# Two transformer blocks on one core: row tests moved to where rows are made, a second query buffer, weight casts on GpSimd, and other places and steps for the Strassen stage's sums, loads and offsets

## The chip, the cores and the metric

The kernel runs on one NeuronCore of a Trainium2 chip. The metric is the device time of one execution in microseconds. Before the change three runs gave a median of 2838.97 us (2838.28 to 2842.82).

## The reference

The input x is 16 sequences of 256 rows with 512 channels, with a context of the same shape. Two blocks follow each other. All arithmetic is in float32.

```python
def block0(x, context, xa_mask):                     # 16 heads of 32
    q = layer_norm(x, qn_w, qn_b) @ q_w
    k, v = split(layer_norm(context, cn_w, cn_b) @ kv_w)
    attn = where(xa_mask, -max, q @ k.T * scale);  attn = softmax(attn)
    x = x + (attn @ v) @ proj_w + proj_b
    h = layer_norm(x, n2_w, n2_b)
    return x + gelu(h @ fc1_w + fc1_b) @ fc2_w + fc2_b    # 512 -> 2048 -> 512

def block1(x, context):
    mask0 = 1.0 - all(x == 0, axis=2)                # per row
    x1 = layernorm(x + mha(x, x, mask0, causal=True))
    mask1 = 1.0 - all(x1 == 0, axis=2)               # per row
    x2 = layernorm(x1 + mha(x1, context, mask1, causal=False))
    z = relu(x2 @ fc1_w.T + fc1_b) * mask0
    return layernorm(x2 + (z @ fc2_w.T + fc2_b) * mask0)
```

In `mha` the mask multiplies Q, K, V and the result, and a number of valid columns is counted from the first row's energies that differ from zero.

## The kernel before

The 16 sequences are worked on as 8 groups (NG) of two sequences, so a group has N = 512 rows, in G = 4 row tiles of 128. A float32 product is made of three matmuls in the format fp32r: every operand is held as a high part (its leading bits, `h`) and a low part (`l` = value - high part), and `mm3` issues high x high, high x low and low x high. The helpers `split`, `split_sb` and `split_lazy` (L119 to L142) make the two parts. In most places ScalarE casts the high part (`nc.scalar.copy`) and VectorE subtracts.

The stages follow each other. Times are of the profiled execution.

- **Phase 1** (to about 711 us): attention of block 0. `Attention.stream` yields, head by head, scores (L409), exponentials (L434, ScalarE, with minima that VectorE made), transposes of the exponentials (L450), their copy to `pt` (L453, ScalarE), and per unit of 4 heads the mixing with V (L466). `weave` interleaves it on PE with a `fill` of projections (`feed`), in proportion to costs that both yield. The last group is woven with `last()`, which also opens the feed forward part: `Mlp0.begin` loads the rows of group 0, normalizes them, makes the first weights and the first operands.
- **Up stage** (about 711 to 1061 us): h @ fc1_w with a seven-product Strassen-Winograd scheme over 2x2 blocks. One step n takes 7 products of 12 matmuls; a group has NS = 4 steps. `sums` makes the four block sums of the operand, `write` puts each of the seven operands as high and low part into one of eight slots as soon as the product that read the slot has been issued. Results go through GELU into `ho` and are stored to DRAM as `hid`.
- **Down stage** (about 1054 to 1458 us): hidden @ fc2_w the same way, 32 steps of 84 matmuls (L1005). In step n, `sums_down(n+1)` makes the sums of the next hidden tile (GpSimd L786 and L788, VectorE L787 and L789) into tile `x2`, which has one buffer; seven `write`s follow between the products; `hidden(n+2)` loads the hidden tile after that (L978), alternately into the tiles `raw` and `x0`. At the first step of a group `residual(g)` loads the group's rows into tile `x1` (L1017) and GpSimd adds the offset `b_fc2` to them (L1018). At the last step `end` adds the seven products into these rows (L1033 to L1050) and stores them (L1052). In the last step of all, `after_up` is called after products 1, 6, 7 and 4; each call loads one row tile of block 1's first group (L1306) and transposes it.
- **Weights of the down stage**: `weigh(2, m)` makes four block differences on GpSimd (L835 to L838, tile `diff`) and splits them, m = 0 to 7. Even m use the `diff` of one pool, odd m that of another. The last two are called just before the down stage.
- **Block 1** (from about 1458 us): self attention of the 8 groups, then cross attention of the 8 groups, then the feed forward part. `front(n, t)` loads a row tile of the job after next (L1306), transposes it, and calls `nonzero` (L1181 to L1186), the row test: VectorE compares 128x512 elements with zero and accumulates a maximum per row, which is the mask. For job 0 `feed(0)` makes these tests. `halves(pool, 0)` gives the buffer `qk0` for one chunk of queries: `split` fills it, `att.keep` stores it to DRAM (L379) so that `build` can load it in the layout of the scores. Chunks of keys have two buffers, those of queries one. `Weight.load` (L174 to L192) loads a chunk of weights, ScalarE casts its high part (L185) and GpSimd subtracts (L186).

Only PE's order is written out by hand (`tc.manual_schedule(engines={PE})`). The other engines' queues and SP's, which issues the DMAs, are put in order when the program is built: the planner follows a model of time, takes an instruction when it becomes ready there, and prefers the one that the program emitted first where several are ready. [...] The pools' tiles wait for the last use of the tile that had the buffer before.

## Time and profile before

The profiled execution took 2842.86 us, of which the span from its first to its last instruction is 2841.0 us.

| | us |
|---|---|
| median of three runs | 2838.97 |
| profiled execution | 2842.86 |
| its span | 2841.0 |
| PE idle in the span | 153.4 |
| row tests L1184: 64, each | 0.68 |
| copies pt L453 of 512 columns: 512, each | 0.595 |
| high parts of weights in block 1 on ScalarE L185, each | 0.62 |

In lines of the profile that list groups or timelines, `out<-in` are the program's names of tiles without buffer numbers, then come the shapes, and in brackets the idle time of the engine just before the instruction and what ended it. A line of waits gives who waited (engine, tile, line), for what, the total time, how often, and the longest. In the lines of stretches each engine has its busy time and its number of instructions; the last three numbers are TensorE's granted clock as a share of full speed, the busy share of the DMA engines, and GB/s.

### The profile page before, as it was taken

What the parts mean: (1) busy time and instruction counts of PE and PEld (TensorE: products, weight loads), DVE (VectorE), ACT (ScalarE), POOL (GpSimd) and SP (SyncE); (2) the same over time, 40 slices, a digit from 0 to 9 for tenths busy, and PEclk for the clock granted to TensorE, in tenths of its full rate; (3) what the DMA queues carried; (4) which work ended last, traced back from release to release, by engine and by line L of the source; (5) the groups of instructions that cost most, each with busy time, mean ns of one, the idle gap of its engine ahead of it and who ended that gap; (6) DMA issues with size and microseconds to landing.
All of it is one profiled execution on the core that took longest, in us unless ns stands there. A gap on an engine that the chain in (4) does not pass through costs nothing.

```text
span 2841.0 us, 56513 instructions
## 1 busy us (share of the span) xinstructions
PE 2687.6 (95%) x18970; PEld 2263.3 (80%) x18970; DVE 2013.1 (71%) x5722; ACT 1840.9 (65%) x5320; POOL 932.9 (33%) x943
## 2 busy tenths in 40 slices
PE   7999999998999989899979999998999999999998
PEld 5777777776899988898977777777777777777787
DVE  7666666757665567787876777776777776776887
ACT  4877777778655553333337777777777777778632
POOL 6122221206311044545441222234333323234533
PEclk9999999999999999999989999999999999999999
DMA  6566565655333343433465556667666665555321
GB/s 228 172 189 186 173 180 170 186 164 151 137 121 133 127 164 132 136 131 138 137 205 176 180 184 186 180 191 216 200 193 186 179 181 177 175 172 169 96 94 60
DMA packets 287664, 465.40 MB, mean 164 GB/s; under 512 B 36240, under 2 KB 188304, under 8 KB 279184
## 3 DMA queue, kind: packets, MB, share of 16 engines
q1 hardware_dynamic: 287376, 461.78, 51.7%
q8 instruction: 153, 2.51, 0.4%
q14 instruction: 135, 1.11, 0.1%
HBM read 284.97 MB, written 176.69 MB: 162 GB/s over the span
## 4 chain that ended last, share of the span: by engine, by line
PE 65%; DMA 11%; DVE 11%; ACT 5%; issue 4%; POOL 2%; SPq 1%; POOLq 0%; ACTq 0%; DVEq 0%
PE ps_v L259 15%; PE ps_p L259 14%; PE ps_pt L450 8%; PE down L1005 6%; PE ps_z L466 5%; PE ps_s L409 4%; PE up_sc L899 4%; DMA x<-xd 3%; PE up_pt L899 3%; ACT e L434 3%; PE up_mm L899 2%; DMA d<-qk 2%; DMA xd<-x 2%; PE ps_t L278 2%; DVE c_t L142 1%
## 5 line engine op out<-in xcount | busy, mean ns | idle before, releaser
L434 ACT ACTIVATE e<-e,mn 128x256 f32<-128x256 f32 (+1 forms) x1024 | 488.2, 481 | 85.1 <-DVE mn L424 83.9
L453 ACT COPY pt<-ps_pt 128x512 f32<-128x512 f32 (+1 forms) x768 | 422.1, 555 | 130.9 <-PE ps_pt L450 124.2
L450 PE MATMUL ps_pt<-ident,e 128*128 128x128 f32 x2816 | 437.0, 273 | 10.4 <-ACT pt L453 9.7
L450 PEld LDWEIGHTS ps_pt<-ident,e 128*128 128x128 f32 x2816 | 336.1, 141 | 52.3 <-ACT pt L453 15.7
L409 PE MATMUL ps_s<-stack 97*128 97x256 f32 (+1 forms) x1536 | 332.8, 298 | 34.2 <-ACT e L434 26.5
L409 PEld LDWEIGHTS ps_s<-stack 97*128 97x128 f32 (+1 forms) x1536 | 267.9, 190 | 98.4 <-ACT e L434 42.7
L1283 POOL TENSOR_TENSOR x<-x,zz 128x256 f32<-128x256 f32 x128 | 95.4, 746 | 593.6 <-DVE zz L1276 565.5
L1005 PE MATMUL down<-w_h,c_t 128*128 128x256 f32 x900 | 265.2, 295 | 24.3 <-DVE c_t L142 24.1
L434 ACT ACTIVATE e<-ps_s,mn 128x256 f32<-128x256 f32 x512 | 244.9, 498 | 65.2 <-DVE mn L420 59.2
L238 POOL TENSOR_TENSOR rstd<-rstd,nhalf 128x1 f32<-128x1 f32 x192 | 127.0, 668 | 472.4 <-DVE rstd L237 425.0
L1005 PE MATMUL down<-w_h,x_t 128*128 128x256 f32 x868 | 254.9, 294 | 18.8 <-ACT x_t L141 18.8
L1005 PE MATMUL down<-w_l,x_t 128*128 128x256 f32 x868 | 253.6, 292 | 0.0
L424 DVE CUSTOM_DVE_ANT_0 e<-mb,ps_s 128x256 f32<-128x256 bf16 x512 | 192.5, 415 | 76.3 <-PE ps_s L409 73.4
L259 PE MATMUL ps_p<-x_t,q_h 128*128 128x512 f32 x640 | 213.9, 415 | 3.2 <-DVE qk L128 3.2
L420 DVE TENSOR_REDUCE mn<-ps_s 128x2 f32<-128x512 f32 x256 | 174.3, 682 | 57.8 <-PE ps_s L409 56.0
L141 ACT CAST x_t<-sums 128x512 fp32r<-128x512 f32 x156 | 93.5, 620 | 178.0 <-DVE sums L787 121.9
L466 PE MATMUL ps_z<-pt,v 128*32 128x256 f32 (+1 forms) x3072 | 201.5, 368 | 5.7 <-ACT pt L453 3.7
L1005 PEld LDWEIGHTS down<-w_h,c_t 128*128 128x128 f32 x900 | 181.9, 202 | 27.8 <-DVE c_t L142 27.8
L434 ACT ACTIVATION_READ_ACCUMULATOR e<-e,mn 128x1 f32 x1024 | 198.5, 194 | 0.0
L1005 PEld LDWEIGHTS down<-w_h,x_t 128*128 128x128 f32 x868 | 175.3, 202 | 20.6 <-ACT x_t L141 20.6
L424 DVE CUSTOM_DVE_ANT_0 e<-tri,ps_s 128x128 f32<-128x128 f32 (+1 forms) x512 | 157.8, 346 | 45.4 <-PE ps_s L409 41.9
L1005 PEld LDWEIGHTS down<-w_l,x_t 128*128 128x128 f32 x868 | 175.2, 202 | 0.0
(242 smaller groups left out, 7515.6 us busy)
## 6 DMA issues: line engine op xcount, KB each, us to landing
stack<-d SPq DMA_DIRECT2D x1152, 128.0 KB
d<-qk SPq DMA_DIRECT2D x192, 512.0 KB
hid<-ho SPq DMA_DIRECT2D x32, 1024.0 KB
raw<-hid SPq DMA_DIRECT2D x32, 1024.0 KB
x<-xd SPq DMA_DIRECT2D x128, 256.0 KB
xd<-x SPq DMA_DIRECT2D x96, 256.0 KB
xin<-in_x_dram SPq DMA_DIRECT2D x32, 256.0 KB
xin<-in_ctx_dram SPq DMA_DIRECT2D x32, 256.0 KB
```

What stands on the lines that cost most here:

```text
L238: nc.gpsimd.tensor_tensor(out=rstd[:, 1:2], in0=rstd[:, 0:1], in1=nhalf, op=ALU.pow)
L259: nc.tensor.matmul(ps, w[p], x[q], start=(k == 0 and i == 0), stop=(k == kc - 1 and i == 2))
L409: nc.tensor.matmul(ps[:, t, :], u.st[: self.rows, 0, j, ts(t, P)], u.st[: self.rows, 1, j, :], start=True, stop=True,)
L420: nc.vector.tensor_reduce(mn, ps, AX.X, ALU.min)
L424: nc.vector.tensor_tensor_reduce(out=e[:, at], in0=bias[t], in1=ps[:, t, : job.width[t]], scale=-SC, scalar=BIG, op0=ALU.add, op1=ALU.min, ...
L434: nc.scalar.activation(e[:, at], ps[:, t, :] if bias is None else e[:, at], AF.Exp, bias=mn[:, t : t + 1], scale=-1.0, accum_out=u.rs[:, t ...
L450: nc.tensor.transpose(pp[:, ts(x, P)], e[:, at : at + P], ident)
L453: nc.scalar.copy(pt[:, :n], pp[:, :n])
L466: nc.tensor.matmul(z[ts(j, D), w[0] * P :], job.v[u.i * NT + mc][:, u.c * P + j * D : u.c * P + (j + 1) * D], u.pt[j][:, x0 * P : (x0 + le ...
L899: nc.tensor.matmul(ps[:, mm, :], w[p][:, k, :], x[q][:, k, :], start=(first and mm == k == j == 0), stop=(k == 1 and j == 2), skip_group_c ...
L1005: nc.tensor.matmul(ps[:, t, :], x[p][:, mm, ts(t, P)], w[r][:, bo, :], start=(q == mm == t == j == 0), stop=(q == self.NS - 1 and mm == 1 ...
L1283: nc.gpsimd.tensor_tensor(out=xv, in0=xv, in1=zz, op=ALU.add)
```

## The change

It makes these edits:

- `Weight.load` can cast the high part on GpSimd (`pooled`); block 1 asks for it for all weights but those of job 0.
- The copy of `pt` goes to VectorE for the heads in `job.shared`: the last head of each unit, in the last group of phase 1 and in all cross jobs.
- `weigh(2, m)` uses the second `diff` only for m = 1. The last two calls move behind steps 0 and 1 of the down stage.
- `write` with an `own` engine (in `begin`) casts the high part on VectorE.
- `normal` is divided into `row` (load) and `normal`. In `begin` all rows are loaded first, with a yield of 12 passes, then normalized, with 3 passes each. In the up stage all four rows of a later group are loaded at step 0 into tile `raw`, and normalized in steps 1 and 2.
- `sums_down(0)` writes into two `xn` tiles and the second `diff` instead of `x2`.
- `residual` (loads) runs in the second step of a group (third for group 0), `offset` (GpSimd's additions) one step later.
- Row tests run in `end`, after the stores, and in `Mha.norm` of self attention, after the layer norm; those in `front` and `feed(0)` are gone.
- In the last down step all row tiles are loaded after product 1 and transposed after products 2, 5, 4 and 3.
- Chunks of queries get two buffers. The third row of the last norm table, fc2's offset, gets a tile of its own.

```diff
             for k in ks:
...
                 if self.gain is None:
-                    nc.scalar.copy(h, raw)
+                    if self.pooled:
+                        nc.gpsimd.tensor_copy(h, raw)
+                    else:
+                        nc.scalar.copy(h, raw)
                     nc.gpsimd.tensor_tensor(out=l, in0=raw, in1=h.bitcast(F32), op=ALU.subtract)
...
-            nc.scalar.copy(pt[:, :n], pp[:, :n])
+            if j in job.shared:
+                nc.vector.tensor_copy(pt[:, :n], pp[:, :n])
+            else:
+                nc.scalar.copy(pt[:, :n], pp[:, :n])
...
-            pool = self.pool if early or m % 2 == 0 else self.tmp
+            pool = self.tmp if not early and m % 2 and (way == 1 or m == 1) else self.pool
             diff = pool.tile([P, 4, 2 * P], F32, tag="diff", name="diff")
...
         def write(self, i, own=None):
-            split_lazy(
-                self.a[i],
-                *[x.rearrange("p (k n) -> p k n", n=self.W) for x in self.next[i]],
-                own or nc.vector,
-            )
+            h, l = [x.rearrange("p (k n) -> p k n", n=self.W) for x in self.next[i]]
+            if own is None:
+                split_lazy(self.a[i], h, l, nc.vector)
+            else:
+                nc.vector.tensor_copy(h, self.a[i])
+                own.tensor_tensor(out=l, in0=self.a[i], in1=h.bitcast(F32), op=ALU.subtract)
...
         def sums_down(self, n):
...
-            s = self.px.tile([P, 4, 2, self.W], F32, tag="x2", name="sums")
-            s = [s[:, i] for i in range(4)]
+            if n == 0:
+                s = [self.up_pool.tile([P, C], F32, tag="xn", name="sums") for _ in range(2)]
+                two = self.tmp.tile([P, 4, 2 * P], F32, tag="diff", name="sums")
+                two = two.rearrange("p (i m) n -> p i m n", m=2)
+                s = [x.rearrange("p (m n) -> p m n", m=2) for x in s] + [two[:, i] for i in range(2)]
+            else:
+                s = self.px.tile([P, 4, 2, self.W], F32, tag="x2", name="sums")
+                s = [s[:, i] for i in range(4)]
...
+            return x
+
+        def offset(self, x):
+            for t in range(G):
                 nc.gpsimd.tensor_tensor(
                     out=x[:, t, :], in0=x[:, t, :], in1=self.b_fc2, op=ALU.add
                 )
-            return x
...
                 for t in range(G):
                     nc.sync.dma_start(out=xd[1][g][ts(t, P), :], in_=x[:, t, :])
+                for t in range(G):
+                    junk = self.flat("junk").rearrange("p m n -> p (m n)")
+                    nonzero(junk, x[:, t, :], m0[:, g, t : t + 1])
...
             for t in range(G):
-                self.normal(0, t, xn[:, t, :])
-                yield 0.0
+                self.row(0, t, xn[:, t, :])
+            yield 12 * PASS
+            for t in range(G):
+                self.normal(xn[:, t, :])
+                yield 3 * PASS
...
-            self.weigh(2, self.NM - 2)
-            self.weigh(2, self.NM - 1)
...
-                if q == 0:
+                if q == (1 if g else 2):
                     xs[g] = self.residual(g)
+                elif q == (2 if g else 3):
+                    self.offset(xs[g])
                 if n + 1 <= last:
                     self.sums_down(n + 1)
...
-                    if n == last and i in (1, 6, 7, 4):
-                        after_up((1, 6, 7, 4).index(i))
+                    if n == last and i in (1, 2, 5, 4, 3):
+                        after_up((1, 2, 5, 4, 3).index(i))
                 self.at = self.next
+                if n < 2:
+                    self.weigh(2, self.NM - 2 + n)
...
                 layer_norm(pool, x, table[:, 0, :], table[:, 1, :], True)
+                if not self.cross:
+                    junk = pool.tile([P, C], F32, tag="t512", name="junk", bufs=3)
+                    nonzero(junk, x, m1[:, self.g, t : t + 1])
...
             x = job.x[:, t, :]
-            nc.sync.dma_start(out=x, in_=xd[2 if job.cross else 1][job.g][ts(t, P), :])
-            cost = transposed(job.x_t, x, t)
-            if n:
-                nonzero(pool, x, job.m[:, t : t + 1])
-            return cost
+            return transposed(job.x_t, x, t)
...
+        def after_up(step):
+            if step:
+                front(0, step - 1, False)
+            else:
+                for t in range(G):
+                    rows_of(0, t)
...
-            if n == 0:
-                for t in range(G):
-                    nonzero(pool, job.x[:, t, :], job.m[:, t : t + 1])
...
-                q, hl = halves(pool, 0)
+                q, hl = halves(pool, 0, 2)
```

`rows_of(n, t)` issues the load that `front` issued, and `front` calls it unless it is told that the rows are loaded already.

## The prediction

> **What bounds the kernel now.** I read the page's engine rows first, then the stretches of stages, the waits, and the timeline around the longest waits.
>
> ```profile
> span 2841.0 us, 56513 instructions
> PE 2687.6 (95%) x18970; PEld 2263.3 (80%) x18970; DVE 2013.1 (71%) x5722; ACT 1840.9 (65%) x5320; POOL 932.9 (33%) x943
> ```
>
> PE is the bound, so a gain can only come out of its gaps: 2841.0 - 2687.6 = 153 us[...]. Where they lie (us, PE, PEld, DVE, ACT, POOL, PEclk):
>
> ```profile
> 640.00:760.00 120.00, 103.93 (x789) 86.90 (x788) 89.99 (x247) 91.17 (x248) 67.30 (x74) 0.99 0.46 145
> 1040.00:1098.00 58.00, 42.71 (x310) 41.40 (x310) 44.45 (x52) 28.83 (x52) 31.66 (x26) 0.85 0.43 146
> 1098.00:1440.00 342.00, 313.17 (x2444) 308.80 (x2442) 274.76 (x308) 123.25 (x215) 175.26 (x118) 0.94 0.39 133
> 1440.00:1500.00 60.00, 48.70 (x254) 40.79 (x253) 39.44 (x102) 17.36 (x31) 18.70 (x21) 0.91 0.70 233
> 1920.00:2040.00 120.00, 105.22 (x759) 83.24 (x758) 85.06 (x367) 89.00 (x303) 54.81 (x51) 0.99 0.73 221
> 2040.00:2680.00 640.00, 611.86 (x4339) 481.27 (x4338) 453.88 (x1128) 488.77 (x1546) 211.74 (x207) 0.99 0.57 170
> ```
>
> Gaps are length less PE busy: 16.1 where phase 1 ends, 15.3 and 28.8 in the Strassen down stage, 11.3 where block 1 starts, 14.8 and 28.1 in cross attention. The last two stages together have 43 of the 153. The waits name the culprits:
>
> ```profile
> POOL x L1018 <- DMA x<-xd: 53.3, 7, 8.5
> DVE junk L1184 <- DMA x<-xd: 35.6, 30, 3.5
> PE ps_s L409 <- ACT e L434: 26.5, 22, 4.2
> ACT qk L127 <- DMA d<-qk: 24.4, 12, 4.0
> ```
>
> Three engines stand in order behind a transfer. GpSimd, in the down stage:
>
> ```profile
> 1124.15 1.29 POOL L786 TENSOR_TENSOR sums<-raw 128x512 f32<-128x512 f32 x1 [2.48 <-issue]
> 1125.40 1.74 POOL L788 TENSOR_TENSOR sums<-raw 128x512 f32<-128x512 f32 x1
> 1135.14 2.54 POOL L1018 TENSOR_TENSOR x<-x,b_fc 128x512 f32<-128x512 f32 x2 [8.00 <-DMA x<-xd]
> 1137.65 1.29 POOL L786 TENSOR_TENSOR sums<-raw 128x512 f32<-128x512 f32 x1
> ```
>
> The sums at 1137.65 wait behind an offset that waits for its load. The first offset of a group starts at 1135.14, 1182.79, 1231.04 and so on to 1372.02: 47.4 us a group. A group's 4 x 84 matmuls stand 0.12 us apart in PE's timeline, 40.3 us: 7 us are lost per group. And VectorE, in cross attention:
>
> ```profile
> 2088.24 0.69 DVE L1184 TENSOR_SCALAR_CACHE_REDUCE junk<-x 128x512 f32<-128x512 f32 x1 [3.46 <-DMA x<-xd]
> 2089.96 0.69 DVE L1184 TENSOR_SCALAR_CACHE_REDUCE junk<-x 128x512 f32<-128x512 f32 x1 [1.03 <-DMA x<-xd]
> 2091.97 0.69 DVE L420 TENSOR_REDUCE mn<-ps_s 128x2 f32<-128x512 f32 x1
> ```
>
> The row test waits for its row, the minimum (L420) behind it, the exponential behind that (at 2092.70, after 3.33 us idle), and PE's scores for 4.24 us until 2093.77.
>
> [...] after 4.42 us idle at 1086.47 matmuls stand 0.21 us apart for 5 us, 2 us lost beyond the gap. [...] L142 takes 0.68 or 1.75 us, all 64 row tests 0.675 to 0.690.
>
> **The change, part by part** (against this execution's span).
>
> *Row tests* (L1184, 64). The pitch is 0.61 us. 32 go from block 1's fronts and feed(0) to the end of down groups, 32 from cross fronts to the self norms. They need no load there. Self attention swaps 28 for 32; there PE's waits of 0.6 to 1.3 us just after each four tests (1598, 1665, 1732, 1800, 1867) go, 5 us.
>
> *Query chunks.* Two buffers end 24.4 us of ScalarE waits in cross and a 3.13 us one at 1927. These and the tests' waits lie side by side (2087.5, 2237.8 and their like), so I don't add them: of the 28.1 us gap I let 14 go, plus 2 us of slow clock for each of two.
>
> *Shared copies.* One in four pt copies, 64 in cross, 8 in phase 1, goes from ScalarE (0.595 us) to VectorE. The trace has no such copy; PSUM-reading L133 takes 0.685[...]. ScalarE's relief shortens other waits of scores: 2 us. Cross in all: -20.
>
> *Weights on GpSimd.* 20 casts (0.62 us each, with waits for their loads) leave ScalarE. A cast on GpSimd: from the 128x256 copy L623 (0.41) 0.8 us, from the one-input L1346 up to 1.57; I take 0.8, and L186 at 1.3 follows each as now. 16 us of GpSimd, in stretches where it is busy under half. Behind it are residual adds and norms whose readers are a group away, so nothing; without cover 1 to 5 us. With the query wait, ScalarE no longer blocks at 1930 to 2000: -7 of 14.8 (between 0 and -12).
>
> *First Strassen sums.* Now sums 0 wants tile x2, so it waits for the store of hidden (1054.32 to 1062.7) and PE for 8.7 us; sums 1 comes late in turn. From 1054 to 1097 pass 43.3 us for 168 down and 36 up matmuls, 24.5 us: 19 lost. Other buffers free sums 0. Against that, odd weight differences share a buffer with even ones: GpSimd's four (0.74 to 1.7 us) wait for VectorE's w_l, some 6 us later per pair, so x0 comes free and hidden 1 loads that much later, and step 1 waits about 5 us. -14 (between -8 and -19). The last two weights' 2 x 2.3 us of VectorE fall within steps 0 to 2, with slack.
>
> *Loads and offsets one and two steps later.* All engines but PE take work in an order planned from readiness, not emission: b_fc, emitted at L1133 just before the down stage, is issued at 709.64. The load stays ready when the group's stores have landed (1131.6), offsets are ready as each row lands, sums not before the last write (1132.6). So the likeliest order is the same: two offsets, then sums. GpSimd still waits. The offset's lower rank helps only where both are ready. SP's order (stores, loads, next hidden) stays. I take 0, between -5 and +1.3 us per group of seven (one more offset ahead).
>
> *Row tests in the down stage.* 4 x 0.61 = 2.4 us per group, just after the last add, before the sums of the next step. VectorE is some 5 us behind PE there (last add 1122.75, PE through at 1117.4), so PE waits 2.4 us more in the next step. The following step waits for the load chain anyway and loses as much less: 0 while the chain stays.
>
> *Start of block 1.* PE waits 5.4 us for x (L1306, issued 1442.85 when x0 is free). The transposes now come two products (2 x 1.44 us) later: -4 with the clock. Then PE waits 3.6 us at 1469 for the second query chunk, split only at 1471.65 behind weight casts and one buffer; the eight tests at 1470 to 1480 go: -4 (between 0 and -7).
>
> *End of phase 1.* ScalarE is 90 to 100% busy. 8 copies and 7 casts leave it (4.8 + 4.3 us). Yields of begin grow by 24 passes, so 24 passes of projection (24 x 0.232 = 5.6 us) fall behind attention's end, alone on PE, while VectorE catches up with weights it is late with at 719 to 734. -3, between -10 and +4.
>
> *Rows of the up stage, tables.* For groups after the first two, four rows are loaded at step 0 into tile raw (256 KB each on SP, ahead of the hidden stores) and normalized a step later, where two were and two followed. PE has 279.12 busy of 280 us from 760 to 1040, so there is nothing to gain; the loads have a step of 10 us before them, and the four bn_stats, 0.69 each, stay as many: 0, and at worst one late row per group, 1 us. The split of the last norm table and fc2_b move no work that anything waits for: 0.
>
> Sum: -5 -20 -7 -14 +0 -8 -3 = -57. The execution itself took 2842.86 (1.9 around its span), 3.9 over the median of the runs; from the median, 2839 - 57 = **2782**.
>
> **Rivals.** *The order turns* (0.28): the offsets fall behind the sums. Then seven groups lose only the tests' 2 us of their 7: -35 more, 2747. For it: sums now rank above offsets and are ready within 2.6 us of the first. Against: readiness, as above. *ScalarE stays the bound in cross* (0.06): exponentials, not blocks, hold PE, and only 5 of 20 come: 2797 to 2810. For it: L434 costs 488+245 us. *VectorE becomes the bound in the down stage, slower* (0.11): it is busy 275 of 342 us. If tests go ahead of writes and these then run at 1.75 us against GpSimd, a group loses 2.4 + 4 x 1.07 + 2 (clock) = 8.7 us over today's 7; with step 0, eight times, 70: 2852. It decides from 7.1 us a group. Against it: 6.3 us idle VectorE before L787 in each.
>
> **How the numbers follow.** The forecast has 0.55: 2782, itself 2762 to 2800. 2738 to 2810 takes in most of the turned order and of the bound ScalarE, and leaves out the slower case. A measurement can tell 0.2%, 5.7 us, from no change. Faster 0.88, same 0.02, slower 0.10.
>
> **What would show it.** L1184 without a wait for x<-xd; L127 without d<-qk; sums L786 of step 0 before 1055; PE's gaps in cross under 15 us. First offsets 47 us apart and waiting: forecast; 42: turned; over 49: VectorE. It is wrong if cross keeps its gaps, or if steps 0 and 1 still take over 38 us.

## The result and the profile after

The changed kernel takes 2833.69 us (median of 16 runs, 2826.16 to 2840.25), the kernel before took 2840.93 us in runs beside it. The ratio is 0.9976, with a 95% interval of 0.9966 to 0.9985: some 7 us faster, where 57 were forecast. The profiled execution has a span of 2832.9 us, 8.1 less than before. Line numbers have shifted: L409 is now L413 (scores), L434 L438 (exponential), L453 L460 (pt copy), L1005 L1025 (down product), L1018 L1042 (offset), L1184 L1225 (row test), L786 and L788 L796 and L798 (sums), L1346 L1409 (mask of the context rows, cx).

The engine rows of the page, which answer to those of before:

```profile
span 2832.9 us, 56614 instructions
...
PE 2683.6 (95%) x18970; PEld 2261.0 (80%) x18970; DVE 2047.1 (72%) x5801; ACT 1794.4 (63%) x5221; POOL 942.1 (33%) x963
```

ScalarE lost 46.5 us of work and VectorE gained 34, as intended. PE is still idle for 149 us. The same six stretches (us, PE, PEld, DVE, ACT, POOL, PEclk). They lie at fixed times, while the changed kernel is up to 25 us behind the other or 19 ahead, so they hold partly other work; the table further down compares equal work:

```profile
640.00:760.00 120.00, 96.47 (x692) 77.63 (x690) 92.53 (x254) 79.16 (x223) 64.79 (x71) 0.94 0.46 136
1040.00:1098.00 58.00, 53.46 (x435) 52.35 (x433) 45.64 (x60) 37.79 (x71) 30.55 (x31) 0.99 0.58 200
1098.00:1440.00 342.00, 312.56 (x2460) 307.71 (x2461) 294.49 (x373) 125.53 (x219) 181.57 (x125) 0.96 0.41 139
1440.00:1500.00 60.00, 56.35 (x327) 48.68 (x327) 42.50 (x102) 22.72 (x48) 23.45 (x25) 0.96 0.70 240
1920.00:2040.00 120.00, 106.30 (x766) 85.68 (x765) 82.87 (x364) 83.74 (x289) 55.78 (x58) 0.94 0.67 204
2040.00:2680.00 640.00, 608.47 (x4291) 478.08 (x4290) 475.32 (x1130) 449.98 (x1445) 227.56 (x223) 0.98 0.55 168
```

Two stretches have clearly smaller gaps (1040 and 1440: the first Strassen sums and the start of block 1). The first has 7.5 us more gap and a PEclk of 0.94 where it was 0.99; the last has 31.5 us of gap where it had 28.1, and cross attention was to give 20. The waits of all engines, longest in total first:

```profile
POOL x L1042 <- DMA x<-xd: 50.4, 7, 8.8
...
PE ps_t L282 <- POOL cx L1409: 24.6, 2, 12.9
...
PE down L1025 <- DVE c_t L142: 24.0, 16, 3.5
...
PE ps_s L413 <- ACT e L438: 13.3, 7, 2.7
...
DVE x L252 <- POOL rstd L242: 12.5, 8, 2.6
...
PE up_sc L912 <- DVE u L968: 8.4, 7, 1.5
...
PE ps_t L880 <- DVE xn L247: 6.3, 1, 6.3
```

What the forecast wanted gone is gone: no row test waits for a row, and ScalarE's wait of 24.4 us for d<-qk at L127 is no more. In its place stand waits that weren't there: PE for cx twice (24.6 us), VectorE for rstd, PE for xn. GpSimd still waits for the offsets' load.

The k-th matmul of a kind is the same matmul in both kernels. Its start after, less its start before, shows where time came and went (us, + is later; the last column is the difference over the stage):

| from, to | shift at the end | forecast | after |
|---|---|---|---|
| start to the fourth up step (751.6 before) | +18.2 | -3 | +18.2 |
| rest of the up stage | +24.1 | 0 | +5.9 |
| first two down steps | +11.9 | -14 | -12.2 |
| other down steps, but the last | +7.4 | 0 | -4.4 |
| last down step, start of block 1 | -3.1 | -8 | -10.5 |
| self attention (to 1898 before) | -10.3 | -5 | -7.3 |
| last self job, start of cross (to 2129) | -4.4 | -7 | +6.0 |
| rest of cross, and to the end | -8.1 | -20 | -3.7 |

Three places went against the forecast: the end of phase 1 with the up stage (27 us), the start of cross (13 us) and cross (16 us). Of the first row +1.6 is there at the first scores. In the other kernels below, whose code and order are the same up to there, this is -0.4 to +3.3. At 635 us it is +4.5 in the changed kernel and -0.1 to +4.8 in the others, so up to 4.5 us of the row may be no effect of the change. Single executions of kernels with the same code also differ in the fourth row (-9.7 to 0.0) and in the fifth (-10.5 to -2.5); in the third (-14.3 to -11.7) and the sixth (-7.8 to -7.1) they agree better.

### The profile page after: what moved, and what is told of

It reads as the page before. It is cut to its first block, busy times and chain, and to the rows that moved or that the text cites. A ratio compares the mean times of both kernels' runs of the same rounds, so it can differ in the third digit from the quotient of the medians.

```text
span 2832.9 us, 56614 instructions
## 1 busy us (share of the span) xinstructions
PE 2683.6 (95%) x18970; PEld 2261.0 (80%) x18970; DVE 2047.1 (72%) x5801; ACT 1794.4 (63%) x5221; POOL 942.1 (33%) x963
## 4 chain that ended last, share of the span: by engine, by line
PE 70%; DVE 13%; DMA 6%; issue 4%; ACT 3%; POOL 3%; SPq 0%; POOLq 0%; DVEq 0%; ACTq 0%
PE ps_p L263 18%; PE ps_v L263 15%; PE ps_pt L454 9%; PE ps_z L473 6%; PE ps_s L413 5%; PE down L1025 5%; PE up_sc L912 4%; DVE c_t L142 3%; PE up_pt L912 2%; PE up_mm L912 2%; PE ps_t L282 2%; ACT e L438 1%; DMA d<-qk 1%; DVE st L238 1%; PE ps_e L1253 1%
## 5 line engine op out<-in xcount | busy, mean ns | idle before, releaser
L438 ACT ACTIVATE e<-e,mn 128x256 f32<-128x256 f32 (+1 forms) x1024 | 487.7, 480 | 69.3 <-DVE mn L428 67.7
L460 ACT COPY pt<-ps_pt 128x512 f32<-128x512 f32 (+1 forms) x696 | 378.0, 546 | 161.8 <-PE ps_pt L454 150.7
L454 PE MATMUL ps_pt<-ident,e 128*128 128x128 f32 x2816 | 437.4, 274 | 11.7 <-ACT pt L460 6.0
L413 PE MATMUL ps_s<-stack 97*128 97x256 f32 (+1 forms) x1536 | 331.7, 297 | 16.8 <-ACT e L438 13.3
L413 PEld LDWEIGHTS ps_s<-stack 97*128 97x128 f32 (+1 forms) x1536 | 269.0, 190 | 72.6 <-ACT e L438 18.3
L438 ACT ACTIVATE e<-ps_s,mn 128x256 f32<-128x256 f32 x512 | 241.0, 483 | 79.1 <-DVE mn L424 50.2
L1025 PE MATMUL down<-w_h,c_t 128*128 128x256 f32 x900 | 261.8, 292 | 24.0 <-DVE c_t L142 24.0
L1025 PE MATMUL down<-w_h,x_t 128*128 128x256 f32 x868 | 252.5, 291 | 9.4 <-ACT x_t L141 7.8
L1025 PE MATMUL down<-w_l,x_t 128*128 128x256 f32 x868 | 251.3, 289 | 0.0
L428 DVE CUSTOM_DVE_ANT_0 e<-mb,ps_s 128x256 f32<-128x256 bf16 x512 | 192.7, 415 | 77.8 <-PE ps_s L413 75.7
L473 PE MATMUL ps_z<-pt,v 128*32 128x256 f32 (+1 forms) x3072 | 212.3, 376 | 10.1 <-DVE zs L651 3.6
L1025 PEld LDWEIGHTS down<-w_h,c_t 128*128 128x128 f32 x900 | 178.3, 198 | 27.6 <-DVE c_t L142 27.6
L438 ACT ACTIVATION_READ_ACCUMULATOR e<-e,mn 128x1 f32 x1024 | 197.8, 193 | 0.0
L1025 PEld LDWEIGHTS down<-w_h,x_t 128*128 128x128 f32 x868 | 172.6, 199 | 11.6 <-ACT x_t L141 9.8
L473 PEld LDWEIGHTS ps_z<-pt,v 128*32 128x32 f32 x3072 | 86.0, 111 | 115.0 <-issue 29.4
```

Source lines behind the costliest of these rows:

```text
L413: nc.tensor.matmul(ps[:, t, :], u.st[: self.rows, 0, j, ts(t, P)], u.st[: self.rows, 1, j, :], start=True, stop=True,)
L428: nc.vector.tensor_tensor_reduce(out=e[:, at], in0=bias[t], in1=ps[:, t, : job.width[t]], scale=-SC, scalar=BIG, op0=ALU.add, op1=ALU.min, ...
L438: nc.scalar.activation(e[:, at], ps[:, t, :] if bias is None else e[:, at], AF.Exp, bias=mn[:, t : t + 1], scale=-1.0, accum_out=u.rs[:, t ...
L454: nc.tensor.transpose(pp[:, ts(x, P)], e[:, at : at + P], ident)
L460: nc.scalar.copy(pt[:, :n], pp[:, :n])
L473: nc.tensor.matmul(z[ts(j, D), w[0] * P :], job.v[u.i * NT + mc][:, u.c * P + j * D : u.c * P + (j + 1) * D], u.pt[j][:, x0 * P : (x0 + le ...
```

## The experiments

All ratios are against the kernel before, in runs beside it on the same chip, with 95% intervals. What is said "by the trace" rests on one execution of each kernel.

### Whose are the two waits of 12 us

The start of cross, in the timeline of the changed kernel (start, duration, engine and line, idle time before it and what ended it; SPq is the queue that issues DMAs):

```profile
1981.14 2.48 POOL L254 TENSOR_TENSOR x<-x,ln 128x512 f32<-128x512 f32 x2
...
1982.43 0.69 DVE L1225 TENSOR_SCALAR_CACHE_REDUCE junk<-x 128x512 f32<-128x512 f32 x1 [1.23 <-POOL x L254]
1982.72 1.26 SPq L1298 DMA_DIRECT2D xd<-x  x2
...
1983.65 0.69 DVE L1225 TENSOR_SCALAR_CACHE_REDUCE junk<-x 128x512 f32<-128x512 f32 x1 [0.53 <-POOL x L254]
1984.04 0.90 SPq L1408 DMA_DIRECT2D cx<-in_ctx_dram  x2
...
1988.15 3.11 POOL L1409 TENSOR_SCALAR cx<-cx,m 128x512 f32<-128x512 f32 x2 [3.31 <-DMA cx<-in_ctx_dram]
...
1989.77 0.48 PE L282 MATMUL ps_t<-ident,cx 128*128 128x128 f32 x1 [11.75 <-POOL cx L1409]
```

PEclk is 0.50 for some 4 us behind each of PE's two waits (from 1989.77 to 1994, from 2065.19 to 2069). The context rows are loaded only once the row tests of the last self norms have run. The tests' unused result `junk` and `cx` are taken from the same ring of three buffers (tag `t512`), in the order of emission: each new tile takes the next buffer and waits for the last use of the tile that had it before. In `front` the tests concerned rows that had been made long before. In `norm` they come after the layer norm, and the loads of `cx` that follow in the ring wait for them, behind the stores on SP too; so reads the timeline. The other suspect is GpSimd's queue, which has the weights' casts in it (v_l before and after this stretch). One kernel for each:

```diff
 a_junk
-                    junk = pool.tile([P, C], F32, tag="t512", name="junk", bufs=3)
+                    junk = pool.tile([P, C], BF16, tag="junk", name="junk", bufs=1)
 b_nopool
-            w[x].pooled = n > 0
+            w[x].pooled = False
```

> After, with the row tests of the self norms writing their unused result to a tile of their own instead of a buffer of the ring of three that the context rows (cx) also use. Theory (the ring): the two PE waits at 1977.7 and 2052.0 (11.9 and 13.1 us, behind cx L1409) are the ring's; they go, with some 2 us of slow clock behind each, so the time falls by 20 to 29 us against the kernel after, to a ratio of about 0.989 to 0.991 against before. Rival (weights on GpSimd fill its queue and delay cx): the time stays within 5 us of after (0.9976) and the wait at 1977.7 stays above 8 us.

> After, with the leading bits of block 1's weights on ScalarE again (pooled False). Rival theory (GpSimd's queue): the first cx wait (11.9 us at 1977.7) goes and the time falls by 10 to 15 us, ratio 0.992 to 0.994. Theory (the ring): both waits stay at 10 us or more, and the time is within 5 us of after, or up to 7 us longer, what the casts were forecast to give: ratio 0.997 to 1.000.

a_junk: 0.9897 (0.9873 to 0.9922), 22 us less than after. (The tile is BF16; a test takes 0.67 us either way. The execution in its trace is 7 us longer than the median of its runs, so differences by the trace against it are some us larger than those of the ratios.) PE doesn't wait for cx any more, and between the scores that stand at 1974.7 and 2129.4 before it gains 12.3 us where the changed kernel lost 14.3. Its timeline has the loads first:

```profile
1980.42 0.35 SPq L1408 DMA_DIRECT2D cx<-in_ctx_dram  x1
...
1983.66 0.41 SPq L1408 DMA_DIRECT2D cx<-in_ctx_dram  x1
...
1984.62 1.57 POOL L1409 TENSOR_SCALAR cx<-cx,m 128x512 f32<-128x512 f32 x1 [0.75 <-PE ps_p L263]
...
1992.17 1.13 SPq L1408 DMA_DIRECT2D cx<-in_ctx_dram  x2
```

b_nopool: 1.0000 (0.9987 to 1.0012), both cx waits still there (21.3 us). So the ring it was. The casts on GpSimd are worth the 7 us that they were forecast at, 1.0000 against 0.9976, uncertain by about 4; by the trace 4 of them are lost in the last self job. The kernels below have the tile of their own, where nothing else is said.

### Copies on VectorE in cross

After that repair cross still gained little: a group takes 76.9 us (mean of six), 77.6 before. In twelve kernels that have the same code and the same order on all engines there, it is 75.7 to 77.3 us in single executions. Its parts:

```diff
 u_oneq
-                q, hl = halves(pool, 0, 2)
+                q, hl = halves(pool, 0)
 v_noshare2                                    (z_share: (HPC - 2, HPC - 1))
-                if cross:
-                    self.shared = (HPC - 1,)
 o_cxact
-            nc.gpsimd.tensor_scalar(cx, cx, job.m[:, t : t + 1], None, ALU.mult)
+            nc.scalar.activation(cx, cx, AF.Copy, scale=job.m[:, t : t + 1])
```

> After with a tile of its own for the norms' tests, and the masks of the context rows applied on ScalarE instead of GpSimd (32 x 0.6 us more on ScalarE). Theory (in cross, GpSimd's cx multiply of 1.57 us stands ahead of the norms' rstd, VectorE waits 12 us for them in six groups, and the minimum and the exponentials behind): VectorE's wait for rstd falls under 5 us, PE's waits of 1.6 to 2.9 us at the start of each group shrink to under 1 us, cross is 6 to 12 us shorter, ratio 0.985 to 0.9875. Rival (ScalarE is the bound there): waits of PE for ACT stay or grow, ratio 0.989 to 0.993.

> After with a tile of its own for the norms' tests, and one buffer for query chunks again. If the second buffer is what shortened self and cross attention (the prediction's 14 of 20 with the tests): ScalarE's waits for d<-qk come back (20 us or more in cross), cross 6 to 12 us longer, ratio 0.992 to 0.994. If the waits lie beside those that remain (the norms' rstd): within 4 us of 0.9897.

> After with a tile of its own for the norms' tests, and the pt copies of cross all on ScalarE again. If ScalarE's relief is worth what the prediction said (2 us): within 4 us of 0.9897, ratio 0.9885 to 0.9915. If ScalarE is the bound in cross: 8 to 25 us longer, ratio 0.9925 to 0.9985.

> After with a tile of its own for the norms' tests, and two of four pt copies of cross on VectorE instead of one. If the copies on VectorE themselves hold cross back: pitch of a group above 78 us, 10 to 30 us more than with one, ratio 0.993 to 1.000. If the loss with one copy is only the order of the work that came with it: pitch between 72 and 77 us, ratio 0.980 to 0.991.

v_noshare2: 0.9803 (0.9787 to 0.9819), 27 us less than a_junk, which neither expectation had; by the trace 22 of them in six groups of cross, which take 73.2 us each (73.3 in y_best below, which has no copies in cross either). The forecast had the copies as a gain of 2. The two kernels' six groups, a_junk first, in stretches as above:

```profile
2107.00:2568.00 461.00, 445.21 (x3169) 349.84 (x3168) 347.48 (x843) 334.37 (x1083) 156.24 (x157) 0.99 0.61 184
```

```profile
2091.00:2530.00 439.00, 435.88 (x3169) 347.72 (x3168) 325.90 (x796) 354.91 (x1132) 155.29 (x157) 1.00 0.63 192
```

Of the 22 us, 13 are gaps (15.8 and 3.1 us) and 9 are a longer busy time of PE for the same number of matmuls (its PEclk is 0.99 and 1.00). VectorE is busy for 75% of the time with the copies: on the mean it had room. The timelines point to the place that a copy takes. The start of a group in a_junk:

```profile
2273.40 0.68 DVE L238 BATCH_NORM_STATS2 st<-x 128x6 f32<-128x512 f32 x1
...
2274.00 0.67 DVE L458 COPY pt<-ps_pt 128x512 f32<-128x512 f32 x1
...
2274.59 0.68 DVE L238 BATCH_NORM_STATS2 st<-x 128x6 f32<-128x512 f32 x1
...
2278.78 1.57 POOL L1409 TENSOR_SCALAR cx<-cx,m 128x512 f32<-128x512 f32 x1 [5.59 <-PE ps_s L413]
...
2280.32 1.19 POOL L242 TENSOR_TENSOR rstd<-rstd,nhalf 128x1 f32<-128x1 f32 x2
...
2280.92 2.20 DVE L252 TENSOR_SCALAR x<-x,mv,rstd 128x512 f32<-128x512 f32 x2 [1.49 <-POOL rstd L242]
...
2283.04 0.68 DVE L424 TENSOR_REDUCE mn<-ps_s 128x2 f32<-128x512 f32 x1
```

And in v_noshare2, a group's start at the same point:

```profile
2249.90 1.28 DVE L238 BATCH_NORM_STATS2 st<-x 128x6 f32<-128x512 f32 x2
...
2252.19 1.07 POOL L242 TENSOR_TENSOR rstd<-rstd,nhalf 128x1 f32<-128x1 f32 x2 [2.50 <-DVE rstd L241]
...
2253.54 0.99 DVE L252 TENSOR_SCALAR x<-x,mv,rstd 128x512 f32<-128x512 f32 x2
```

As these timelines read, a copy between the two statistics makes the norm's rstd (one over the standard deviation) late, and the planner, which goes by readiness, puts the mask of the context row (1.57 us) ahead of it on GpSimd. VectorE then waits for rstd in every group (10.7 us in six; none before), its scaling runs beside GpSimd's product (2.20 us for two instead of 0.99), and the minimum, the exponential and PE's next scores come after it. In the trace of the changed kernel L252 takes 0.53 us (at most 0.544) where GpSimd is idle, 16 times, and up to 1.58 where L253 runs beside it, 31 times, which agrees. o_cxact takes the mask off GpSimd and leaves the copies: 0.9852 (0.9833 to 0.9871). VectorE's wait for rstd is gone, PE's for the exponential fell from 12.3 to 3.1 us, and the six groups are 8.8 us shorter than a_junk's (75.4 us each, just below the spread of the twelve). That is less than half of the 22, so a part of the copies' loss isn't in this wait.

z_share, with two copies of four: 0.9907 (0.9879 to 0.9936), 77.7 us a group; its wait for rstd is 10.0 us. The time of a group falls between the two expectations, the ratio within the second. The first copy costs 3.7 us a group, the second 0.9, which isn't clear of the spread: mostly a step, as the turned order on GpSimd would have it, and not a price per copy. PE's own order is the same in the traces of all three kernels, so the loss is in what PE waits for. How the part outside the wait for rstd comes about wasn't settled.

u_oneq: 0.9944 (0.9929 to 0.9959), so the second query buffer is worth 13 us (uncertain by 8), but not in cross: with one buffer the six groups are 1.5 us shorter than a_junk's. 8 of the 13 are in self attention, up to the scores at 1898 before: a_junk gains 7.8 us there on before, u_oneq nothing (+0.2). Where the rest is the traces don't show. ScalarE's waits with one buffer, in self attention and then in cross:

```profile
ACT qk L132 <- DMA d<-qk: 22.5, 13, 3.6
...
ACT qk L127 <- DMA d<-qk: 6.4, 8, 2.1
```

In a_junk, with two buffers, neither stretch lists such a wait. Before the change the wait in cross was 24.4 us, so most of it goes without the second buffer too.

### The end of phase 1 and the up stage

The residual rows (xr, L679) and the rows that the up stage loads next come late in the changed kernel. GpSimd's timeline, after and then before:

```profile
700.34 1.28 POOL L861 TENSOR_TENSOR c_t<-xt,x_t 128x512 fp32r<-128x512 f32 x1 [3.85 <-DVE x_t L860]
...
718.44 1.29 POOL L861 TENSOR_TENSOR c_t<-sums,x_t 128x512 fp32r<-128x512 f32 x1 [0.36 <-DVE x_t L860]
721.85 1.29 POOL L679 TENSOR_TENSOR xr<-xr,b_o 128x512 f32<-128x512 f32 x1 [2.11 <-DMA xr<-in_x_dram]
```

```profile
683.34 1.28 POOL L142 TENSOR_TENSOR c_t<-xt,x_t 128x512 fp32r<-128x512 f32 x1 [4.69 <-ACT x_t L141]
...
698.86 2.68 POOL L142 TENSOR_TENSOR c_t<-sums,x_t 128x512 fp32r<-128x512 f32 x2
...
708.33 1.29 POOL L669 TENSOR_TENSOR xr<-xr,b_o 128x512 f32<-128x512 f32 x1
```

`begin`'s seven writes start 17 us later. They end 2 us before the first up matmul, 9 us before it in the kernel before, with the residual rows' offsets among and behind them. Six kernels undo the parts here:

```diff
 c_noshare1 (without the own tile)
...
-                if g == NG - 1:
-                    self.shared = (HPC - 1,)
 j_begin: both of the next two
 q_yields
                 self.row(0, t, xn[:, t, :])
-            yield 12 * PASS
-            for t in range(G):
                 self.normal(xn[:, t, :])
-                yield 3 * PASS
+                yield 0.0
 r_casts: in write
-            if own is None:
-                split_lazy(self.a[i], h, l, nc.vector)
-            else:
-                nc.vector.tensor_copy(h, self.a[i])
-                own.tensor_tensor(out=l, in0=self.a[i], in1=h.bitcast(F32), op=ALU.subtract)
+            split_lazy(self.a[i], h, l, own or nc.vector)     # ScalarE casts
 k_up
...
-                        load(g + 1)
+                        for t in range(2):
+                            load(g + 1, t)          # load and normal, as before
                     elif s <= 2:
-                        for t in (2 * s - 2, 2 * s - 1):
-                            self.normal(xn[t])
...
 x_diff
-            pool = self.tmp if not early and m % 2 and (way == 1 or m == 1) else self.pool
+            pool = self.pool if early or m % 2 == 0 else self.tmp
```

> After, with no pt copies on VectorE in phase 1 (8 copies back on ScalarE). Theory (VectorE is late at the end of phase 1, and PE waits behind L458): PE's waits for pt L458 there (six of 0.8 to 2.5 us between 670 and 710, 9.9 us) go and no equal wait on ScalarE comes back; first up matmul 6 to 10 us earlier than in after (721.87), time 5 to 9 us less, ratio 0.9945 to 0.996. Rival (ScalarE was the bound there, as the prediction said): first up matmul no earlier or up to 5 us later, ratio 0.9976 or above.

> After with a tile of its own for the norms' tests, and the up stage's begin as before the change (rows loaded and normalized at once, no further passes between, leading bits of its writes on ScalarE). Theory (the longer begin pushes GpSimd's first writes behind the last attention, and the last residual rows and first weights behind them): first up matmul at 711 to 716 us instead of 723.4, and the PE wait for xn (6.1 us) shrinks or goes; 8 to 14 us less, ratio 0.985 to 0.987. Rival (the lateness comes from the pt copies on VectorE or from the rows of the up stage): first up matmul within 3 us of 723.4, ratio 0.9885 to 0.991.

> After with a tile of its own for the norms' tests, and of begin only the order and the passes between as before the change (rows normalized at once, no 24 added passes); leading bits of its writes stay on VectorE. Theory (the added passes make it late): nearly all of what the whole begin gave (ratio 0.982, 22 us) comes: first up matmul within 3 us of the 720.4 of the run with the old begin, no long wait for xn, ratio 0.982 to 0.9845. Rival (the casts on VectorE, each in two instructions with GpSimd waiting for it, make it late): ratio 0.987 to 0.990.

> After with a tile of its own for the norms' tests, and of begin only the leading bits of its seven writes back on ScalarE. Theory (the passes): within 4 us of the run with the tile alone, ratio 0.988 to 0.9905, xn wait of 5 us or more stays. Rival (the casts): ratio 0.982 to 0.985.

> After with a tile of its own for the norms' tests, and the up stage's rows loaded and normalized as before the change (two at a time in tiles xn, at the places where they were). Theory (four rows are normalized at steps 1 and 2 ahead of the adds of those steps): the wait up_sc <- DVE u of 1.66 us at each of groups 2 to 6 goes (7 us in all) and the wait for xn shrinks; 7 to 13 us less, ratio 0.985 to 0.9875. Rival (the prediction's term, nothing, since VectorE's adds are late for another reason): the waits stay, ratio 0.989 to 0.991.

> After with a tile of its own for the norms' tests, and the buffers of the weight differences as before the change (odd ones apart from even ones). Prediction's term: GpSimd waits for VectorE's w_l from then on, some 6 us late per pair. If that delays the first up steps: the wait of 4.1 us at 736 goes and the up stage is 3 to 8 us ahead; if the first Strassen sums need the place (their second tile takes it): first two down steps 4 to 8 us longer. Sum between -6 and +6 us, ratio 0.9875 to 0.992.

| kernel | ratio | interval | first up matmul at | seventh up step, later than before by |
|---|---|---|---|---|
| a_junk | 0.9897 | 0.9873 to 0.9922 | 723.4 | 19.7 |
| j_begin | 0.9820 | 0.9803 to 0.9836 | 720.4 | 6.9 |
| q_yields | 0.9848 | 0.9823 to 0.9872 | 722.4 | 11.0 |
| r_casts | 0.9863 | 0.9843 to 0.9883 | 717.2 | 14.2 |
| k_up | 0.9854 | 0.9840 to 0.9867 | 718.9 | 14.0 |
| x_diff | 0.9897 | 0.9881 to 0.9912 | 720.0 | 15.6 |
| c_noshare1 | 0.9960 | 0.9944 to 0.9975 | 716.8 | 11.0 |

The first matmul says little, since single executions differ by up to 7.1 us there with the same code (718.9 to 726.0). A difference of two ratios against a_junk is uncertain by about 8 us, against after by 5.

`begin` costs 22 us. Of its parts the passes have 14 and the casts 10, so neither expectation was met; with the uncertainty of 8 the casts' share is hardly shown. Behind the first matmul only the passes show: from there to the seventh up step every kernel with them loses 5 to 9 us on before, r_casts 7.9, while q_yields and j_begin gain 0.5 and 2.5. Rows 2 and 3 of group 1 come late (PE waits 6.3 us for xn from 755 in the changed kernel, 0.4 in j_begin).

The rows of the up stage cost 12 us by the ratios. By the traces 7 of them come after the seventh up step: to the 31st every kernel with the new rows loses 7.0 to 7.2 us more, every one with the old rows at most 0.1. PE's wait for u, from 760 to 1060, in after, before and k_up:

```profile
PE up_sc L912 <- DVE u L968: 6.9, 6, 1.5
...
PE up_sc L899 <- DVE u L955: 1.8, 4, 0.5
...
PE up_sc L912 <- DVE u L968: 0.7, 2, 0.5
```

In after the norms of two rows a step stand ahead of the adds.

The 8 copies of phase 1 cost 4.5 us against after's 0.9976, which is within the uncertainty; the trace has PE's waits for pt between 640 and 760, on either engine, at 8.2 us in after and 4.8 in c_noshare1. The buffers of the differences (x_diff) give nothing in sum: without the sharing the first two down steps are 6.4 us longer, and that execution has it back in later down steps. m_ph1up undoes c_noshare1, j_begin, k_up and x_diff together:

> After with a tile of its own for the norms' tests, and four parts of the change undone together: pt copies of phase 1 on ScalarE, the begin of the up stage, its rows, and the buffer of the weight differences, each as before. If the parts' losses add up (6 to 10, 8 to 14 with some of the same time in both, 7 to 13, 0 to 3): first up matmul at 709 to 713 us, up stage without the shift, 18 to 26 us less in all, ratio 0.981 to 0.984. Rival (they undo the gain of the first Strassen sums with them, since the order of all engines hangs together): 5 to 12 us less, ratio 0.9855 to 0.988.

0.9807 (0.9789 to 0.9826), 26 us. The up stage then runs 1.5 us behind before, and the first two down steps gain only 5.2. The parts alone sum to 39 us (22, 12 and 4.5), so their losses overlap; that each removes a part of the same late start is the likely reading.

### Row tests and offsets in the down stage

```diff
 d_tests (without the own tile): in end
-                for t in range(G):
-                    junk = self.flat("junk").rearrange("p m n -> p (m n)")
-                    nonzero(junk, x[:, t, :], m0[:, g, t : t + 1])
 d_tests: in front, and for job 0 in feed
+            if n and not job.cross:
+                test(n, t)
 p_turned: in residual, which the later groups now call in q == 1, after sums_down(n + 1)
...
+                nc.vector.tensor_copy(x[:, :, 0], after[:, 0, 0:G])      # after = self.a[3]
```

> After, with the row tests of the self jobs back at the start of block 1's jobs (none at the end of down groups). Theory (the tests stand in VectorE's order ahead of the next step's writes and sums and PE waits for them): the waits of 0.9 + 1.4 us per group at the first step of each of seven groups (1143 to 1419) go, the down stage from 1109.16 to 1440 is 10 to 17 us shorter, self attention loses 5 to 7 us again; time 4 to 12 us less, ratio 0.9935 to 0.996. Rival (prediction's term: tests in the down stage cost nothing, the load chain holds PE anyway): down stage within 3 us of after, time 3 to 8 us more, ratio 0.9985 to 1.0005.

> After with a tile of its own for the norms' tests, and the load of the residual rows of groups 1 to 7 in the down stage made to wait for the first sum of the next step (a copy of 4 numbers per partition into its tile), so that GpSimd's order is sums, then all four offsets. Theory (the prediction's rival, the order turns: sums behind offsets cost a group most of what it loses): PE's waits of 1.2 to 3.7 us at the second step of a group (1158, 1202, 1247, 1296, 1387, 1431) go, the pitch of a group falls from about 45 to 42.5 to 43.5 us, 11 to 18 us in all: ratio 0.983 to 0.986. Rival (only the tests and writes on VectorE hold PE now, or offsets collide with writes instead): pitch within 1 us of after's, ratio 0.988 to 0.992.

d_tests: 1.0028 (1.0018 to 1.0039), 15 us more than after; by the trace 7 of them are in the down stage (third step to the last) and 4 in self attention. The first theory fell: the tests do cost PE 0.8 + 1.3 us at the first step of a group, but without them a group took 47.1 us, as before the change (47.25), and with them 45.7. (In eleven other kernels with that order of the down stage it is 44.8 to 46.5; all these are means of five groups.) The prediction's term wasn't right either. What differs is the next step: without the tests PE waits 2.5 us or more there in each of the seven groups (2.75 us up to 1304.3, after 1.24 up to 1301.1), with them in one to five of seven, and less in the others (in the changed kernel 0.36 and 1.25, then 1.76 up to 1297.7). Why that wait becomes shorter with more work on VectorE wasn't settled.

The clock isn't shown to be the reason. Matmuls at half the clock (0.21 us apart, not 0.12) cost 13.7 us over seven groups without the tests and 9.6 with them, but 5 to 14 us in the kernels with the same order. How long PE waited doesn't tell where the clock falls either: in u_oneq a lone wait of 1.73 us, up to 1294.5, was followed by matmuls 0.21 us apart for 3.4 us, while in a_junk one of 2.75 us, up to 1254.5, was followed by matmuls 0.12 us apart. In the changed kernel two waits of 0.78 and 1.26 us (up to 1330.51) had matmuls 0.21 us apart behind them, one of 1.76 us (up to 1297.72) matmuls 0.12 us apart.

p_turned: 0.9861 (0.9847 to 0.9875), 10 us less than a_junk (uncertain by 8), where the rival of the forecast had 35. The ratio is at the edge of the theory's range, the time of a group between theory and rival. GpSimd now takes the sums first, in the changed kernel two offsets:

```profile
1288.09 2.54 POOL L1042 TENSOR_TENSOR x<-x,b_fc 128x512 f32<-128x512 f32 x2 [7.27 <-DVE c_t L142]
1290.58 1.30 POOL L796 TENSOR_TENSOR sums<-raw 128x512 f32<-128x512 f32 x1
```

```profile
1281.52 1.27 POOL L798 TENSOR_TENSOR sums<-raw 128x512 f32<-128x512 f32 x1
1286.20 6.71 POOL L1044 TENSOR_TENSOR x<-x,b_fc 128x512 f32<-128x512 f32 x4 [3.40 <-DVE c_t L142]
1292.87 1.28 POOL L796 TENSOR_TENSOR sums<-raw 128x512 f32<-128x512 f32 x1
```

A group takes 45.0 us here and 44.4 in the three versions below, against 44.8 to 46.5, 45.6 on the mean, in twelve kernels with the old order. With 40.3 at full speed (336 matmuls 0.12 us apart), the order of the offsets had about 1 of the 5 us that a group loses, not most of them. PE's remaining waits are for VectorE's writes and adds (16.6 us; VectorE is busy 306 of 342 us) and for ScalarE's casts (6.1).

### Together

> After with a tile of its own for the norms' tests, begin and rows of the up stage and pt copies of phase 1 as before the change, and the loads of the down stage behind the sums (the turned order); buffers of the weight differences as in after. If the gains add up (22 for begin, up to 8 more for rows and copies, 10 for the order): 2765 to 2777 us, ratio 0.975 to 0.979. If a shared limit takes them back (the end of phase 1 or the first Strassen sums), 0.979 to 0.983.

> The version with the own tile, begin, rows and phase 1's copies as before and the turned order (ratio 0.978), and besides the context rows' masks on ScalarE. If the gain in cross (9 us, PE's wait for the exponential 12.3 to 3.1 us) adds to the others: 2764 to 2774 us, ratio 0.9735 to 0.977. If not: 0.977 to 0.980.

> The version with the own tile, begin, rows and phase 1's copies as before and the turned order (ratio 0.978), and the pt copies of cross all on ScalarE. If the 22 us that these gave in cross (six groups at 72.2 instead of 76.5 us) add to the others: 2751 to 2761 us, ratio 0.969 to 0.9725. If the versions share a limit in cross: 0.974 to 0.978.

s_best (j_begin, k_up, c_noshare1 and p_turned): 0.9781 (0.9764 to 0.9798). w_all (and o_cxact): 0.9782 (0.9766 to 0.9797), no gain: by the trace its six groups of cross are 4.4 us shorter, but 2.5 us are lost in the last self job and 2.4 at the start of cross, all of it within what single executions differ by. y_best (s_best with v_noshare2): 2759.52 us, **0.9723** (0.9695 to 0.9751), 79 us faster than before. Its last two stretches:

```profile
1920.00:2040.00 120.00, 119.16 (x861) 95.86 (x859) 90.95 (x339) 97.26 (x325) 56.36 (x57) 1.00 0.73 215
2040.00:2680.00 640.00, 634.05 (x4358) 503.45 (x4358) 486.80 (x1117) 467.24 (x1441) 238.90 (x233) 1.00 0.55 167
```

Of the 43 us of gaps in them before, 7 are left; counted between the same matmuls in both kernels it is 42.9 and 7.4.

## Why the prediction was wrong

The direction was right, the size was not: 57 us forecast, 7 measured, outside the range. Of the change's parts, these were right:

- **First Strassen sums**, -14: -12.2. PE's wait of 8.7 us for the store of hidden is gone.
- **Weights on GpSimd**, -7: 7 us by b_nopool. A cast took 0.61 us, under the 0.8 assumed.
- **Start of block 1**, -8: -10.5, and -2.5 to -10.5 in other kernels with the same code, so the number isn't settled.
- **Order of the offsets**: it did not turn, and GpSimd waits 50.4 us for their load as it did. What failed here is the reading behind it, that a group's 7 us are lost behind that load: where the order was turned (p_turned), about 1 us a group went.

These failed:

- **Row tests, "They need no load there"** (22 us by a_junk). True of the rows, but the step looked at what a moved instruction reads and costs and not at what it writes. Its result is never used, yet it holds a place in a ring that loads of the next stage use.
- **Shared copies, -2** (27 us the other way). The forecast counted the price of the instruction, and that price on VectorE was not shown: the trace before has no such copy. After, one takes 0.68 us (L458, 72 of them), on ScalarE 0.59. What the runs show in its place is 3.7 us a group, a part of it by a copy's place in VectorE's queue, ahead of a chain (rstd, scaling, minimum): o_cxact, which breaks that chain, wins back less than half. VectorE's mean load, 453.88 of 640 us before and 475.32 after, was taken as cover and was none.
- **Row tests in self attention, -5, and query chunks, 14 in cross**: self attention came out near the number (-7.3) by luck, since the tests alone were to do it and it took both edits. With one query buffer nothing of the gain is left (u_oneq), with the tests put back 3.1 us of it (d_tests). The buffer's gain was put in cross, where ScalarE's waits for d<-qk were longest. They ended there, mostly without the second buffer, and PE had nothing of it. Without the copies the six groups are 26 us faster than before: the 20 were there to be had. Whether the buffer helps in cross once the copies are gone wasn't tried.
- **End of phase 1, -3, between -10 and +4** (22 for begin and 4.5 for the copies, +18.2 in the trace). The bound counted the added passes as PE's work, 5.6 us. What the traces show in its place: GpSimd's sums and writes are late, these stand in its queue ahead of the last residual rows (their offset at 721.85, 708.33 before), and the next rows are loaded behind the stores of those.
- **Rows of the up stage, 0, at worst 1** (12 us, 7 of them by the traces behind the seventh step). "PE has 279.12 busy of 280" was taken as nothing to gain; there was something to lose. The norms now come ahead of the adds that PE waits for.
- **Row tests in the down stage, 0**: they cost PE some 2 us, as was said, and a group got about 1.5 us shorter all the same. In the trace of the changed kernel the next step's wait is shorter by more than they cost; why stays open.

The slower rival (VectorE as bound in the down stage) and the bound ScalarE did not come. What the slower one says of writes against GpSimd the trace before shows in kind: L142 of 128x512 takes at most 0.69 us where GpSimd is idle and up to 1.84 where it works beside it. Losses and gains almost cancelled, and none of the rivals had that, for all kept the gains whole. Two readings in the working are off without bearing on this: from 1054 to 1097 there are 24 up matmuls, not 36, so 20 us are lost, not 19; and PE's waits just after the tests of self attention are 0.4 to 1.0 us, 3.7 in all and not 5.

## What to carry to other kernels

An instruction that moves takes its output with it: list the buffer ring it writes to and who comes next in that ring, even where nobody reads the result. Before calling work on another engine covered, look at the one chain in that engine's queue that starts each unit of work; here a mean load of 75% did not cover a copy that landed in it. And a stage in which PE is busy throughout is no place where an edit is free: the up stage, with 279.12 of 280 us busy, lost 12.

## What the runs showed that was not expected

- More work on VectorE made the down stage's groups shorter (about 2 us more for PE to wait in the first step, 45.7 against 47.1 us a group). The cause is open.
- How long PE waited didn't settle whether its clock fell: after a lone wait of 1.73 us in u_oneq it did, after one of 2.75 us in a_junk it didn't.
- One copy in four cost 3.7 us a group, two in four 4.5.
- Where code and order of the down stage are the same, a group took 44.8 to 46.5 us in single executions: differences of a few us between two profiles there are not the change's.
